# The first image's projection and convolution as a phase of their own in SBUF

## The chip, the cores and the metric

The kernel runs on one NeuronCore of one Trainium2 chip. The core has five engines that run side by side and wait for each other through semaphores: TensorE (PE), VectorE (DVE), ScalarE (ACT), GpSimd (POOL) and SyncE (SP), which here only issues DMAs. Each engine takes its own instructions strictly in the order in which the program gives them. The metric is device time in microseconds (us); the time before is the median of five runs.

## The reference

Two layers on an image batch x of 8 x 192 x 64 x 64 (float32). The second one is a window attention with an MLP and is not touched. The first, cut to what matters:

```
x = conv1x1(x, W_in)                          # 192 -> 384 channels
x = depthwise_conv3x3(x, W_dw) + b_dw         # each of the 384 channels by itself, 'SAME'
x_proxy = conv1x1(x, W_xd)                    # 384 -> 16
ws, Ls, Us, Ds = (conv1x1(x_proxy, w) for w in (W_w, W_l, W_u, W_d))
xs = concat of x, x transposed, and both flipped along W       # four directions
Gl, Gm, Gr = parts of ws, divided by the sum of their absolute values
out = gate_scan(xs, Ls, Gl, Gm, Gr, chunk=8)  # h = l*x + gl*h_up + gm*h + gr*h_dn, 8 steps
y = sum over directions of w_m * (out * Us + xs * Ds); layernorm; grn; conv1x1(y, W_out)
```

The change concerns the first two lines for image 0 alone.

## The kernel before, in words

All data are float32 and 128 partitions hold 128 channels: the 384 channels are three tiles, `ct` 0 to 2. An image is handled in three parts.

*front* (L526 to L641) makes the convolved image. It goes through the image in eight strips of eight rows (`s`). `read` (L530) loads two strips of x into `xt`. `project` (L541) multiplies by `w_in` on PE, ACT copies the result to `xin` (L561), and SP stores that to a zero-bordered copy of the image in DRAM, `pad` (L570). `convolve` (L575) loads `strip` tiles from `pad`, so that three image rows' worth of 32 channels lie on 96 partitions (L584), and PE multiplies them by the banded matrix `w_cv` (L596). ACT writes the outcome twice with the bias added: `st` (L610), in the order in which the forward scan takes its columns, and `sn` (L623), plain. SP stores them to two DRAM arrays, `xs` (L629) and `xsT` (L630). An image has 24 such blocks (3 tiles by 8 strips).

*scan* (L644 to L1041) takes one image in eight steps t. For each step `proxy` (L659) loads `x0` from `xs` (L662), multiplies by `w_xd` on PE (L669), copies (L679), sends the result to DRAM and back to spread it over the partitions (`flat` L684, `xe` L692), and copies it in the other order (`xo` L699). Then 12 tiles (four directions by three `ct`) are worked off by PE (gate products, L709), ACT (L766, L788, L810, L812), DVE (L742 at t = 0, later L758, L773, L775, L807, L825, L834, L842; outputs L868, L873) and POOL (L797, L814, L818, L829; sums L880, L882, L888, L890). Every step reads all of its image's `xs`; `xd` loads (L725) take columns of `xs` and `xsT`.

*windows* (L1563) is the second layer on the finished image.

The order is written out by a planner (`Plan`, L78 to L308). Each part declares its steps with an engine, a cost in ns, what it reads and writes, and a rank (a due time); `order` (L146) simulates the five engines 60 times with shifted ranks and keeps the shortest run; the instructions are then emitted in that order under a manual schedule (L1587 to L1592). The loop at L1577 gives the scan of image b, the windows of image b-1 and the front of image b+1 to the planner, so that they interleave; the front of image 0 has nothing beside it but the weights' preparation.

Before the planner's part stand the loads of weights (`load`, L332, on SP's and ACT's queues by turns), zeroed buffers (`blank`, L344, on DVE), the zero rows of `pad` (L398, SP) and the preparation of the weights (L403 to L476): `w_cv` (L408 to L410), `w_g2` by `w_m` (L419), `w_out` (L422 to L425), two bias rows (`bias_row`, L427, whose DMAs L431, L442 and L444 go by SP), `b_f1` and `w_f1` (L466 to L472), `rpb`. These lie outside of the manual schedule; there the framework's own scheduler orders them. L485 loads ACT's function table.

Of the kernel before, what the change touches and what calls it, by code (L numbers as in the profile page):

```python
# [23 lines left out]
F32 = mybir.dt.float32  # L24
U8 = mybir.dt.uint8
AF = mybir.ActivationFunctionType
ALU = mybir.AluOpType
AX = mybir.AxisListType
PSUM = bass.MemoryType.PSUM
DRAM = bass.MemoryType.DRAM  # L30

P = 128
B, DM, H, W = 8, 192, 64, 64
DIN, ND, NS = 384, 4, 16
CT = DIN // P
CH = 8
HEADS, HD, WS = 6, 32, 8
HALF = DM // 2
NG = H // WS
# [15 lines left out]
class Held:  # L55
# [5 lines left out]
        self.users, self.left, self.end, self.next, self.tile = [], 0, 0.0, None, None  # L61

    def make(self):
        pool, shape, dtype, name, tag, bufs = self.args
        self.tile = pool.tile(shape, dtype, name=name, tag=tag, bufs=bufs)

# [250 lines left out]
def tile_ss2d_then_window_attention(ctx: ExitStack, tc: tile.TileContext, a: dict, out: bass.AP):  # L317
# [6 lines left out]
    nc = tc.nc  # L324
    x = a["x"]
# [6 lines left out]
    def load(name, src=None, rows=None):  # L332

        nonlocal n_loads
        src = a[name] if src is None else src
        shape = list(src.shape)
        t = const.tile([rows or shape[0]] + shape[1:], F32, tag=name, name=name)
        if rows:
            nc.vector.memset(t[HALF:rows], 0.0)
        queues[n_loads % 2].dma_start(t[0 : shape[0]], src)  # L340
        n_loads += 1
        return t

    def blank(name, shape, value=None):  # L344
        t = const.tile(shape, F32, tag=name, name=name)
        if value is not None:
            nc.vector.memset(t, value)
        return t

    w_in = load("w_in")  # L350
    vecs = load("vecs")
    w_xd = load("w_xd")
    w_g1 = load("w_g1")
    w_g2 = load("w_g2")
# [12 lines left out]
    b_f1 = load("b_f1")  # L367
    w_f2 = load("w_f2")
    b_f2 = load("b_f2")
    b_dw, gamma, beta, ln_w, ln_b = (vecs[:, k, :] for k in range(5))  # L370
    n2_g, n2_b = (n2_gb[:, k, :] for k in range(2))

    ident = blank("ident", [P, P])
    make_identity(nc, ident)
    mean384 = blank("mean384", [P, RG], 1.0 / DIN)
    eps5 = blank("eps5", [P, 1], 1e-5)
    eps7 = blank("eps7", [P, 1], 1e-7)
    neg = blank("neg", [P, 1], NEG)
# [9 lines left out]
    xT = blank("xT", [P, 2, GT])  # L388
    sT, oT = (blank(n, [P, 2, GT], 0.0) for n in ("sT", "oT"))
    for t in (sT, oT):  # L390
        nc.vector.memset(t[HALF : HALF + 1, 1, :], 1.0)

    dram = ctx.enter_context(tc.tile_pool(name="dram", bufs=2, space=DRAM))

    pad = [dram.tile([DIN, H + 2, W + 2], F32, name=f"pad{k}", bufs=1) for k in range(2)]
    for k in range(2):
        for row in (0, H + 1):
            nc.sync.dma_start(  # L398
                pad[k][:, row, :].rearrange("(n p) w -> p n w", p=P), hid[0][0][:, 0 : CT * (W + 2)].rearrange("p (n w) -> p n w", n=CT)
            )  # L400


    with tc.tile_pool(name="prep", bufs=2) as prep, tc.tile_pool(name="prep_ps", bufs=2, space=PSUM) as prep_ps:  # L403

# [11 lines left out]
        for n, pair in enumerate(PAIRS):  # L416
            for k, (d, _) in enumerate(pair):
                w = w_g2[64 * k : 64 * k + 64, n * P : (n + 1) * P]
# [30 lines left out]
        for j in range(2):  # L449
            ps = prep_ps.tile([P, 512], F32, name="ps_pre")  # L450
            for ci in range(2):
                nc.tensor.matmul(
                    ps[0:HALF, 0:1],
                    lhsT=w_v[0:HALF, ci, j * HALF : (j + 1) * HALF],
                    rhs=n1_b[:, ci : ci + 1],
                    start=ci == 0,
                    stop=ci == 1,
# [5 lines left out]
        for m in range(NM):  # L463
            cols = slice(m * P, (m + 1) * P)
# [5 lines left out]
        for ci in range(2):  # L470
            w = w_f1[:, ci, :]
# [15 lines left out]
    plan = Plan()  # L487
# [1075 lines left out]
    def windows(b, z, made):  # L1563
        for g in range(NG):
            yield from window_row(b, g, z, *made[b])

    def written_down(b, lane, length, ahead, steps):

        plan.lane = lane
        k = 0  # L1570
        plan.rank = b - ahead
        for _ in steps:
            k += 1
            plan.rank = b + min(1.0, k / length) - ahead

    made, scans, sums = {}, {}, {}
    for b in range(-1, B + 1):  # L1577
        if 0 <= b < B:
            sums[b] = Held(dram, [P, CT, CH, 512], "z")
            written_down(b, 0, CH * 12 + 1, 0.4, scan(b, *scans[b], sums[b], made))  # L1580
        if 0 <= b - 1 < B:
            written_down(b, 1, NG * 25, 0.0, windows(b - 1, sums[b - 1], made))
        if b + 1 < B:
            scans[b + 1] = tuple(Held(dram, [P, CT, CH, 512], n, bufs=3) for n in ("xs", "xsT"))
            written_down(b, 2, CT * 12, 0.5, front(b + 1, *scans[b + 1]))

    kinds = mybir.EngineType  # L1587
    with tc.manual_schedule(engines={kinds.PE, kinds.Activation, kinds.DVE, kinds.Pool, kinds.SP}):
        for s in plan.order():
            for h in s.makes:  # L1590
                h.make()
            s.fn()  # L1592


def _laid_out(i):

    z = lambda *s: np.zeros(s, np.float32)
    f = lambda n: np.asarray(i[n])
    rows = lambda a, n: np.ascontiguousarray(a.reshape(-1, n, a.shape[-1]).transpose(1, 0, 2))
    cols = lambda a, n: np.ascontiguousarray(a.reshape(-1, n).T)  # L1600
    L0, L1 = "L0_conv_", "L1_conv_"

    w_xd = z(P, CT, RG)
    w_g1, w_g2 = z(P, ND * DIN), z(P, len(PAIRS) * P)
    w_xd[:, :, 0:NS] = rows(f(L0 + "W_xd").T, P)
    gates = f(L0 + "W_w").reshape(3, ND * DIN, NS)
    for r, w in enumerate([gates[0], gates[1], gates[2], f(L0 + "W_l")]):
        w_g1[RG * r : RG * r + NS] = w.T
    for n, pair in enumerate(PAIRS):
        for k, (d, ct) in enumerate(pair):  # L1610
            chs = slice(d * DIN + ct * P, d * DIN + (ct + 1) * P)
            for m, w in enumerate(("W_d", "W_u")):
                w_g2[64 * k + RG * m :][:NS, n * P : (n + 1) * P] = f(L0 + w)[chs].T


    qkv_w = f(L1 + "qkv_w").reshape(3, 3, 2, HD, DM).transpose(0, 2, 1, 3, 4)
    qkv_b = f(L1 + "qkv_b").reshape(3, 3, 2, HD).transpose(0, 2, 1, 3)
    proj = f(L1 + "proj_w").reshape(DM, 3, 2, HD).transpose(2, 1, 3, 0)

    at = np.stack(np.meshgrid(np.arange(WS), np.arange(WS), indexing="ij")).reshape(2, -1)  # L1620
    at = at.reshape(2, WS, WS).transpose(0, 2, 1).reshape(2, -1)
    rel = at[:, :, None] - at[:, None, :] + WS - 1
    rpb = f(L1 + "rpb_table")[rel[0] * (2 * WS - 1) + rel[1]]
    rpb = rpb.reshape(64, 64, 3, 2).transpose(3, 0, 2, 1).reshape(P, 3, 64)

    vec = [f(L0 + n) for n in ("b_dw", "grn_gamma", "grn_beta", "ln_w", "ln_b")]
    twice = lambda a: np.stack([a[0:P], np.concatenate([a[P:DM]] * 2)], 1)
    laid = {
        "x": f("x"),
        "w_in": twice(f(L0 + "W_in").T),  # L1630
        "w_dw": f(L0 + "W_dw").reshape(CT, 4, RG, 3, 3).transpose(3, 2, 0, 1, 4).reshape(3 * RG, CT * 12),
        "vecs": np.stack([cols(v, P) for v in vec], 1),
        "w_xd": w_xd,
        "w_g1": w_g1,
        "w_g2": w_g2,
        "w_m": f(L0 + "w_m"),
        "w_out": rows(f(L0 + "W_out").T, P),
        "w_qk": rows(qkv_w[:2].reshape(2 * DM, DM).T, HALF),
        "b_qk": qkv_b[:2].reshape(1, 2 * DM),
        "w_v": rows(qkv_w[2].reshape(DM, DM).T, HALF),  # L1640
        "b_v": cols(qkv_b[2].reshape(DM), HALF),
        "w_pr": rows(proj.reshape(DM, DM), HALF),
        "b_pr": f(L1 + "proj_b").reshape(1, DM),
        "n1_g": f(L1 + "norm1_g"),
        "n1_br": f(L1 + "norm1_b").reshape(1, DM),
        "n1_b": cols(f(L1 + "norm1_b"), HALF),
        "n2_gb": np.stack([twice(f(L1 + n)) for n in ("norm2_g", "norm2_b")], 1),
        "temp": f(L1 + "temperature").reshape(3, 2).T.reshape(HEADS),
        "rpb": rpb,
        "w_f1": twice(f(L1 + "fc1_w").T),  # L1650
        "b_f1": cols(f(L1 + "fc1_b"), P),
        "w_f2": rows(f(L1 + "fc2_w").T, P),
        "b_f2": twice(f(L1 + "fc2_b")),
    }
    return {k: np.ascontiguousarray(v) for k, v in laid.items()}
# [17 lines left out]
```

## Time and profile before

| what | value |
|---|---|
| median of 5 runs (lowest to highest) | 7635.64 us (7619.77 to 7638.28) |
| the profiled execution | 7638.28 us, span 7636.5 us |
| mean granted PE clock over the span | 0.862 |
| PE busy | 6713.8 us (88%) |
| DVE busy | 6283.7 us (82%) |
| POOL busy | 6212.1 us (81%) |
| ACT busy | 4887.9 us (64%) |

Times in a view of the trace count from the start of the span. A line of the timeline gives start, duration, engine, source line, operation, what is written and read, how often, and in brackets how long the engine had been idle and what ended that. "PEld" is PE loading weights and "SPq" SP issuing a DMA. A line of grouped instructions gives count, total and mean duration (ns), and then the idle time just before them with what ended most of it.

### The profile page before, as it was taken

The page shows a single profiled execution, that of the slowest core. Times are in us where ns is not written, and L with a number is a line of the kernel's source. Part 1 is how long each engine was busy: PE and PEld are TensorE (multiplying, and loading weights), DVE is VectorE, ACT ScalarE, POOL GpSimd, SP SyncE. Part 2 cuts the span into 40 slices and gives each one's busy share as a digit, 9 for nine tenths or more (in the row PEclk, how much of TensorE's full clock was granted, in tenths as well). Part 3 has the DMA queues.
Part 4 walks back from the last instruction along what each step waited for, and adds up shares of the span by engine and source line. Part 5 has one row for each costly group of instructions (what it writes and reads, how often), then busy time and mean ns, then how long its engine had stood idle before and what let it go on. Part 6 is the DMA issues. An engine that isn't in the chain of part 4 may idle for free.

```text
span 7636.5 us, 144071 instructions
## 1 busy us (share of the span) xinstructions
PE 6713.8 (88%) x51224; PEld 3465.8 (45%) x51224; DVE 6283.7 (82%) x15421; ACT 4887.9 (64%) x9657; POOL 6212.1 (81%) x6302
## 2 busy tenths in 40 slices
PE   6788888998998999899999899998888888888887
PEld 2333344444444444444444444444444444444554
DVE  1387889899899988899889979889899999999543
ACT  2355546776677666776677657767566656767665
POOL 0388989899899989888889979888889989899422
PEclk8788779988898889988899789988888788889998
DMA  7766545411552145411553135511211212111100
GB/s 189 186 174 164 137 117 139 122 50 58 147 146 74 47 117 134 126 48 51 139 151 86 43 89 148 134 48 50 61 49 43 58 52 59 45 49 48 30 22 14
DMA packets 1037924, 695.49 MB, mean 91 GB/s; under 512 B 704115, under 2 KB 860214, under 8 KB 1037206
## 3 DMA queue, kind: packets, MB, share of 16 engines
q1 hardware_dynamic: 1035830, 684.99, 33.8%
q8 instruction: 406, 6.65, 0.4%
q14 instruction: 312, 2.56, 0.1%
q10 hardware_dynamic: 1376, 1.30, 0.1%
HBM read 453.43 MB, written 232.67 MB: 90 GB/s over the span
## 4 chain that ended last, share of the span: by engine, by line
PE 22%; DVE 19%; POOL 14%; ACT 8%; issue 4%; DMA 1%; SPq 0%; POOLq 0%; ACTq 0%; DVEq 0%
PE g L709 7%; PE lp L1528 4%; POOL pw L829 2%; POOL ab L797 2%; POOL pw L814 2%; PE lp L1494 2%; POOL dx L882 2%; DVE rest L1281 2%; POOL pw L818 1%; DVE nb L807 1%; DVE nb L834 1%; PE lp L596 1%; PE lp L1137 1%; POOL y L890 1%; DVE dx L868 1%
## 5 line engine op out<-in xcount | busy, mean ns | idle before, releaser
L709 PE MATMUL g<-xo,w_g 32*128 32x512 f32 x3648 | 1232.0, 735 | 210.0 <-DVE dx L868 78.8
L709 PE MATMUL g<-xe,w_g 32*128 32x512 f32 x3648 | 1159.6, 749 | 170.2 <-DVE dx L868 46.1
L766 ACT ACTIVATE ab<-g 128x512 f32<-128x512 f32 x1344 | 781.2, 596 | 387.3 <-PE g L709 157.2
L797 POOL TENSOR_TENSOR ab<-ab 128x512 f32<-128x512 f32 x672 | 868.8, 1293 | 137.2 <-ACT ab L766 125.0
L829 POOL TENSOR_TENSOR pw<-pw,rr 128x512 f32<-128x512 f32 x672 | 867.0, 1290 | 132.9 <-ACT rr L812 107.5
L814 POOL TENSOR_TENSOR pw<-pw,pq 128x512 f32<-128x512 f32 x672 | 875.4, 1303 | 83.0 <-DVE pq L773 66.5
L818 POOL TENSOR_TENSOR pw<-pw,pq 128x512 f32<-128x512 f32 x672 | 874.0, 1301 | 14.6
L882 POOL TENSOR_TENSOR dx<-dx,hu 128x512 f32<-128x512 f32 x576 | 742.1, 1298 | 119.8 <-DVE hu L873 101.6
L810 ACT ACTIVATE rr<-nb,eps 128x512 f32<-128x512 f32 x672 | 460.6, 685 | 556.6 <-DVE nb L807 554.5
L596 PE MATMUL lp<-strip,w_cv 128*32 128x256 f32 x9216 | 669.7, 432 | 114.0 <-DMA strip<-pad 103.6
L709 PEld LDWEIGHTS g<-xo,w_g 32*128 32x128 f32 x3648 | 417.8, 208 | 759.9 <-DVE dx L868 184.8
L709 PEld LDWEIGHTS g<-xe,w_g 32*128 32x128 f32 x3648 | 407.1, 212 | 651.9 <-DVE dx L868 136.0
L1528 PE MATMUL lp<-hd,w_f 128*64 128x256 f32 (+1 forms) x2304 | 578.9, 488 | 45.6 <-ACT hd L1514 15.3
L890 POOL TENSOR_TENSOR y<-y,dx 128x512 f32<-128x512 f32 x384 | 598.6, 1565 | 2.1
L825 DVE SCALAR_TENSOR_TENSOR nb<-nb,rr 128x512 f32<-128x512 f32 x672 | 466.3, 694 | 124.0 <-ACT rr L812 121.8
L834 DVE SCALAR_TENSOR_TENSOR nb<-nb,pw 128x512 f32<-128x512 f32 x672 | 466.0, 694 | 120.9 <-POOL pw L829 118.8
L880 POOL TENSOR_TENSOR y<-hu,dx 128x512 f32<-128x512 f32 x192 | 249.6, 1305 | 379.2 <-DMA xsT<-sn 278.3
L807 DVE TENSOR_TENSOR nb<-nb,ab 128x512 f32<-128x512 f32 x672 | 466.6, 694 | 107.9 <-POOL ab L797 100.4
L596 PEld LDWEIGHTS lp<-strip,w_cv 128*32 128x32 f32 x9216 | 299.0, 121 | 503.2 <-issue 262.1
L873 DVE TENSOR_TENSOR hu<-g,hid 128x512 f32<-128x512 f32 x768 | 521.0, 684 | 5.6 <-PE g L709 4.3
L788 ACT ACTIVATE nb<-nb 128x512 f32<-128x512 f32 x672 | 399.2, 594 | 160.5 <-DVE pq L773 87.1
L709 PE MATMUL nb<-xe,w_g 32*128 32x512 f32 x672 | 477.7, 797 | 19.7 <-DVE hid L842 19.3
(205 smaller groups left out, 16688.0 us busy)
## 6 DMA issues: line engine op xcount, KB each, us to landing
strip<-pad SPq DMA_DIRECT2D x1152, 132.0 KB
xd<-xsT SPq DMA_DIRECT2D x384, 256.0 KB
pad<-xin SPq DMA_DIRECT2D x192, 264.0 KB
xsT<-sn SPq DMA_DIRECT2D x192, 256.0 KB
xs<-st SPq DMA_DIRECT2D x192, 256.0 KB
xd<-xs SPq DMA_DIRECT2D x192, 256.0 KB
x<-xs SPq DMA_DIRECT2D x64, 768.0 KB
z<-y SPq DMA_DIRECT2D x64, 768.0 KB
```

The source lines that it names most:

```text
L596: nc.tensor.matmul(pc()[q * RG : (q + 1) * RG, k * 256 : (k + 1) * 256].rearrange("p (h w) -> p h w", h=4), lhsT=w_cv[:, ct, q, dx, :], rh ...
L709: nc.tensor.matmul(dst, lhsT=w[rows, col : col + P], rhs=xp[rows, :], start=True, stop=True)
L766: lambda r=r: nc.scalar.activation(ab()[:, r, :], g[r](), AF.Abs),
L797: plan("POOL", gp(512), lambda: nc.gpsimd.tensor_add(ab()[:, 0, :], ab()[:, 0, :], ab()[:, 1, :]), w=[ab])
L807: plan("DVE", vec(512), lambda: nc.vector.tensor_add(nb(), nb(), ab()[:, 0, :]), r=[ab], w=[nb])
L814: plan("POOL", gp(512), lambda: nc.gpsimd.tensor_add(one(), one(), pq()[:, 0, :]), r=[(pq, 0)], w=[pw])
L818: lambda: nc.gpsimd.tensor_add(one(), one(), pq()[:, 1, :]),
L829: plan("POOL", gp(512), lambda: nc.gpsimd.tensor_mul(one(), one(), rr()), r=[rr], w=[pw])
L834: lambda: nc.vector.scalar_tensor_tensor(nb(), nb(), 2.0, one(), ALU.subtract, ALU.mult),
L882: plan("POOL", gp(512), lambda: nc.gpsimd.tensor_add(dx(), dx(), hu()), r=[hu], w=[dx])
L890: nc.gpsimd.tensor_add(y, y, dx().rearrange("p (c i) -> p i c", c=CH))
L1528: nc.tensor.matmul(dst[:, at : at + rhs.shape[-1]], lhsT=lhsT, rhs=rhs, **flags)
```

## The change

Image 0 leaves the planner. Its front is written out by hand as a phase that runs before everything else but the loads:

- All of image 0's x is loaded into two tiles, `xa` (channels 0 to 127) and `xb` (the other 64, in two halves of the partitions), in four units of 16 rows, on SP (`xa`) and ACT (`xb`); all weight loads but `w_in`, `w_dv` (the nine taps as a scalar per channel, a new input) and `vecs` come after these.
- `projected` does the product with `w_in` for 16 rows and copies them into `full[ct]`, an image of 66 x 66 with zero borders, in SBUF.
- `convolved` does a block of 16 rows on DVE: one tensor_scalar with the bias, eight multiply-adds onto `acc`.
- `convolved_by_products` does it on PE: nine products with a diagonal matrix `dg` for each half of the block, summed in PSUM, then ACT adds the bias.
- `stored` copies a block into `sn` and `st` on ACT and stores them; blocks are twice as high as before, so a store carries 512 KB and not 256.
- Of 12 blocks, nine go to DVE (ct 0, ct 1, and the first of ct 2), three to PE (the rest of ct 2).

The zeroing of buffers moves from DVE to POOL. The manual schedule now covers the whole program, the weights' preparation too, which keeps its place in the text and so follows the phase on each engine. The planner starts with scan 0 and has seven fronts.

```diff
-            nc.vector.memset(t[HALF:rows], 0.0)
+            nc.gpsimd.memset(t[HALF:rows], 0.0)
...
-    def blank(name, shape, value=None):
+    def blank(name, shape, value=None, engine=nc.gpsimd):
...
-            nc.vector.memset(t, value)
+            engine.memset(t, value)
...
+    ctx.enter_context(tc.manual_schedule(engines={kinds.PE, kinds.Activation, kinds.DVE, kinds.Pool, kinds.SP}))
...
+    ident = blank("ident", [P, P])
+    make_identity(nc, ident)
+
     w_in = load("w_in")
-    vecs = load("vecs")
+    w_dv = load("w_dv")
+    xa = epool.tile([P, H, W], F32, name="xa")
+    xb = epool.tile([P, NG // 2, 8, W], F32, name="xb")
+    for u in range(NG // 2):
+        nc.sync.dma_start(xa[:, 16 * u : 16 * u + 16, :], x[0, 0:P, 16 * u : 16 * u + 16, :])
+        for k in range(2):
+            row = 16 * u + 8 * k
+            nc.scalar.dma_start(xb[64 * k : 64 * k + 64, u], x[0, P:DM, row : row + 8, :])
+        if u == 0:
+            vecs = load("vecs")
+    full = [epool.tile([P, H + 2, W + 2], F32, name=f"full{ct}") for ct in range(CT)]
+    for t in full:
+        nc.vector.memset(t[:, 0 : H + 2 : H + 1, :], 0.0)
+        nc.vector.memset(t[:, :, 0 : W + 2 : W + 1], 0.0)
...
+    with early, tc.tile_pool(name="early_ps", bufs=2, space=PSUM) as early_ps:
...
+        def projected(ct, u):
+            cols = slice(ct * P, (ct + 1) * P)
+            pin = early_ps.tile([P, 16, W], F32, name="pin")
+            outs = [pin[:, 8 * k : 8 * k + 8, :] for k in range(2)]
+            for k in range(2):
+                row = 16 * u + 8 * k
+                nc.tensor.matmul(outs[k], lhsT=w_in[:, 0, cols], rhs=xa[:, row : row + 8, :], start=True, stop=False)
+            for k in range(2):
+                half = slice(64 * k, 64 * k + 64)
+                nc.tensor.matmul(outs[k], lhsT=w_in[half, 1, cols], rhs=xb[half, u], start=False, stop=True)
+            nc.scalar.copy(full[ct][:, 16 * u + 1 : 16 * u + 17, 1 : W + 1], pin)
+
+        def stored(ct, u, acc):
+            cols = slice(128 * u, 128 * u + 128)
+            xs, xsT = scans[0]
+            st, sn = (epool.tile([P, CH, 2, 64], F32, name=n, bufs=3) for n in ("st", "sn"))
+            nc.scalar.copy(sn.rearrange("p t k w -> p k t w"), acc.rearrange("p (k t) w -> p k t w", k=2))
+            nc.sync.dma_start(xsT()[:, ct, :, cols], sn.rearrange("p t k w -> p t (k w)"))
+            for k in range(2):
+                rows = acc[:, 8 * k : 8 * k + 8, :]
+                nc.scalar.copy(
+                    st[:, :, k, :].rearrange("p t (r c) -> p r c t", c=CH), rows.rearrange("p r (c t) -> p r c t", t=CH)
+                )
+            nc.sync.dma_start(xs()[:, ct, :, cols], st.rearrange("p t k w -> p t (k w)"))
+
+        def near(ct, u, dy, dx):
+            return full[ct][:, 16 * u + dy : 16 * u + dy + 16, dx : dx + W]
+
+        def convolved(ct, u):
+            acc = epool.tile([P, 16, W], F32, name="acc", bufs=3)
+            for n, tap in enumerate(taps):
+                w = w_dv[:, ct, n : n + 1]
+                if n == 0:
+                    nc.vector.tensor_scalar(acc, near(ct, u, *tap), w, b_dw[:, ct : ct + 1], ALU.mult, ALU.add)
+                else:
+                    nc.vector.scalar_tensor_tensor(acc, near(ct, u, *tap), w, acc, ALU.mult, ALU.add)
+            stored(ct, u, acc)
+
+        def convolved_by_products(ct, u):
+            acc = epool.tile([P, 16, W], F32, name="acc", bufs=3)
+            for k in range(2):
+                pc = early_ps.tile([P, CH, W], F32, name="pc")
+                for n, (dy, dx) in enumerate(taps):
+                    row = 16 * u + 8 * k + dy
+                    nc.tensor.matmul(
+                        pc, lhsT=dg[:, n, :], rhs=full[ct][:, row : row + 8, dx : dx + W], start=n == 0, stop=n == 8
+                    )
+                nc.scalar.activation(acc[:, 8 * k : 8 * k + 8, :], pc, AF.Identity, bias=b_dw[:, ct : ct + 1])
+            stored(ct, u, acc)
+
+        for n in range(9):
+            nc.scalar.activation(dg[:, n, :], ident, AF.Copy, scale=w_dv[:, CT - 1, n : n + 1])
+        units = [(ct, u) for ct in range(CT) for u in range(NG // 2)]
+        by_vector = [(ct, u) for ct, u in units if ct < CT - 1 or u == 0]
+        by_tensor = [c for c in units if c not in by_vector]
+        done = 0
+        for ct, u in units:
+            projected(ct, u)
+            while done < len(by_vector) and by_vector[done] < (ct, u):
+                convolved(*by_vector[done])
+                done += 1
+            while by_tensor and by_tensor[0] < (ct, u):
+                convolved_by_products(*by_tensor.pop(0))
+        for c in by_tensor:
+            convolved_by_products(*c)
...
+    plan("SP", (0.0, 0.0), lambda: None, w=scans[0])
...
-            written_down(b, 2, CT * 12, 0.5, front(b + 1, *scans[b + 1]))
+            if b >= 0:
+                written_down(b, 2, CT * 12, 0.5, front(b + 1, *scans[b + 1]))
```

More of the change, by code (lines that the diff above doesn't have):

```diff
@@ L63, in make @@
     def make(self):
+        if self.tile is not None:
+            return
         pool, shape, dtype, name, tag, bufs = self.args
@@ L342, in load @@
         return t
-    def blank(name, shape, value=None):
+    def blank(name, shape, value=None, engine=nc.gpsimd):
         t = const.tile(shape, F32, tag=name, name=name)
         if value is not None:
-            nc.vector.memset(t, value)
+            engine.memset(t, value)
         return t
-    w_in = load("w_in")
-    vecs = load("vecs")
+    kinds = mybir.EngineType
+    ctx.enter_context(tc.manual_schedule(engines={kinds.PE, kinds.Activation, kinds.DVE, kinds.Pool, kinds.SP}))
+    dram = ctx.enter_context(tc.tile_pool(name="dram", bufs=2, space=DRAM))
+    scans = {b: tuple(Held(dram, [P, CT, CH, 512], n, bufs=3) for n in ("xs", "xsT")) for b in range(B)}
+    early = ExitStack()
+    epool = early.enter_context(tc.tile_pool(name="early", bufs=1))
+    ident = blank("ident", [P, P])
+    make_identity(nc, ident)
+    w_in = load("w_in")
+    w_dv = load("w_dv")
[12 more added lines that the diff above has]
+        nc.vector.memset(t[:, :, 0 : W + 2 : W + 1], 0.0)
+    b_dw = vecs[:, 0, :]
     w_xd = load("w_xd")
@@ L369, in tile_ss2d_then_window_attention @@
     b_f2 = load("b_f2")
-    b_dw, gamma, beta, ln_w, ln_b = (vecs[:, k, :] for k in range(5))
+    gamma, beta, ln_w, ln_b = (vecs[:, k, :] for k in range(1, 5))
     n2_g, n2_b = (n2_gb[:, k, :] for k in range(2))
-    ident = blank("ident", [P, P])
-    make_identity(nc, ident)
     mean384 = blank("mean384", [P, RG], 1.0 / DIN)
@@ L390, in tile_ss2d_then_window_attention @@
     for t in (sT, oT):
-        nc.vector.memset(t[HALF : HALF + 1, 1, :], 1.0)
-    dram = ctx.enter_context(tc.tile_pool(name="dram", bufs=2, space=DRAM))
+        nc.gpsimd.memset(t[HALF : HALF + 1, 1, :], 1.0)
     pad = [dram.tile([DIN, H + 2, W + 2], F32, name=f"pad{k}", bufs=1) for k in range(2)]
@@ L400, in tile_ss2d_then_window_attention @@
             )
+    for h in scans[0]:
+        h.make()
+    with early, tc.tile_pool(name="early_ps", bufs=2, space=PSUM) as early_ps:
+        taps = [(dy, dx) for dy in range(3) for dx in range(3)]
+        dg = epool.tile([P, 9, P], F32, name="dg")
+        def projected(ct, u):
[58 more added lines that the diff above has]
+            convolved_by_products(*c)
+        assert done == len(by_vector)
@@ L1574, in written_down @@
             plan.rank = b + min(1.0, k / length) - ahead
-    made, scans, sums = {}, {}, {}
+    made, sums = {}, {}
+    plan("SP", (0.0, 0.0), lambda: None, w=scans[0])
     for b in range(-1, B + 1):
@@ L1583, in tile_ss2d_then_window_attention @@
         if b + 1 < B:
-            scans[b + 1] = tuple(Held(dram, [P, CT, CH, 512], n, bufs=3) for n in ("xs", "xsT"))
-            written_down(b, 2, CT * 12, 0.5, front(b + 1, *scans[b + 1]))
[L1587 to L1592, printed above, removed]
+            if b >= 0:
+                written_down(b, 2, CT * 12, 0.5, front(b + 1, *scans[b + 1]))
+    for s in plan.order():
+        for h in s.makes:
+            h.make()
+        s.fn()
 def _laid_out(i):
@@ L1630, in _laid_out @@
         "w_in": twice(f(L0 + "W_in").T),
+        "w_dv": rows(f(L0 + "W_dw").reshape(DIN, 9), P),
         "w_dw": f(L0 + "W_dw").reshape(CT, 4, RG, 3, 3).transpose(3, 2, 0, 1, 4).reshape(3 * RG, CT * 12),
```

## The prediction

> **What bounds the kernel now.** I read the page's forty slices first, then busy time by stretch around the start, then the waits of the first 400 us, then the timeline there.
>
> ```profile
> DVE  1387889899899988899889979889899999999543
> POOL 0388989899899989888889979888889989899422
> ```
>
> One slice is 191 us. VectorE and GpSimd are near nine tenths from the third slice on and almost idle in the first and half of the second: a start stage that only PE, ACT and the DMAs work in.
>
> ```profile
> 27.15:248.07 220.92, 141.06 (x1284) 64.09 (x1280) 3.71 (x17) 54.56 (x74) 0.00 (x0) 0.80 0.77 195
> 248.07:275.88 27.81, 18.74 (x141) 7.96 (x144) 0.00 (x0) 5.98 (x10) 0.00 (x0) 0.69 0.61 165
> 275.88:960.00 684.12, 583.58 (x3998) 245.55 (x3995) 530.88 (x837) 360.31 (x615) 583.33 (x461) 0.78 0.61 161
> ```
>
> Busy us of PE, PE loads, DVE, ACT, POOL, then clock, DMA share, GB/s. In the first stretch (image 0's front) DVE works 3.7 of 221 us, while the DMA engines are 0.77 busy with the trip through the padded copy in DRAM. Only after 275.88 do the scan's engines fill up.
>
> ```profile
> POOL y L880 <- DMA xsT<-sn: 278.3, 1, 278.3
> DVE hid L742 <- PE g L709: 250.4, 4, 241.3
> ```
>
> Both scan engines sit through one wait of 240 to 280 us. It is exposed from end to end.
>
> ```profile
> 244.53 0.37 SPq L629 DMA_DIRECT2D xs<-st  x1
> 248.07 0.60 SPq L662 DMA_DIRECT2D x<-xs  x1
> ...
> 260.01 0.64 SPq L684 DMA_DIRECT2D flat<-xq  x1
> ...
> 263.19 0.57 SPq L692 DMA_DIRECT2D xe<-flat  x1
> ...
> 275.88 0.69 DVE L742 TENSOR_TENSOR hid<-g,x 128x512 f32<-128x512 f32 x1 [241.35 <-PE g L709]
> ```
>
> The last store of image 0, the first load of the scan 3.5 us later, then 27.8 us of proxy chain to the first scan product. That chain and all behind it stay. So the change is worth the move of one event, the issue of the scan's first x0 load, at **248.07 us** now.
>
> **Rows that price the new phase.** VectorE:
>
> ```profile
> 1013.58 0.70 DVE L834 SCALAR_TENSOR_TENSOR nb<-nb,pw 128x512 f32<-128x512 f32 x1 [2.45 <-POOL pw L829]
> 1014.31 0.69 DVE L842 TENSOR_TENSOR hid<-lx,nb 128x512 f32<-128x512 f32 x1
> 1014.92 0.68 DVE L868 TENSOR_TENSOR dx<-g,xd 128x512 f32<-128x512 f32 x1
> 1015.52 0.68 DVE L873 TENSOR_TENSOR hu<-g,hid 128x512 f32<-128x512 f32 x1
> ```
>
> Independent 512-wide operations start 0.60 us apart; L842 needs L834's result and starts 0.73 after it. Another 512 elements cost 0.53 us (L926, 1536 wide, takes 1.751 against 0.694: 1.057 for 1024). A tap is 1024 wide and adds onto the tap before it: 0.73 + 0.53 = 1.26 us. Bounds: 1.13 as if independent; 1.31 with an allowance of 0.05 for the scalar read per partition, which no row isolates.
>
> The Trainium skill, "VectorE: DVE Perf Modes", section Terms, has the pipe emptied after every operation before the next may issue. The row contradicts it for independent operations, 0.60 apart at 0.68 long. By the rule a tap would take its whole 1.22 us, or 0.04 us less than I take; over 72 taps 3 us less.
>
> The first tap has one tensor source. L472 halves its rate per element (768 in 0.60, 192 in 0.30): 1024 in 0.73, taken 0.75.
>
> ```profile
> 40.88 0.50 PEld L550 LDWEIGHTS lp<-xt,w_in 128*128 128x128 f32 x2 [0.81 <-issue]
> 41.90 0.34 PEld L550 LDWEIGHTS lp<-xt,w_in 128*128 128x128 f32 x1 [0.52 <-issue]
> ...
> 238.78 0.30 PEld L550 LDWEIGHTS lp<-xt,w_in 128*128 128x128 f32 x2 [0.41 <-ACT sn L623]
> 239.32 0.19 PEld L550 LDWEIGHTS lp<-xt,w_in 128*128 128x128 f32 x1 [0.24 <-issue]
> ```
>
> A 128x512 product is two passes. Loads of one kind come 0.85 us apart after idle time and 0.43 in busy stretches, so a product takes 1.71 (slow) to 0.86 us (fast).
>
> ```profile
> L610 ACT ACTIVATE st<-lp,vecs 128x512 f32<-128x512 f32 x192 | 223.0, 1162 | 72.3 <-PE lp L596 64.6 <-issue 4.7 <-ACT xin L561 1.8
> L699 ACT COPY xo<-xe 128x512 f32<-128x512 f32 x64 | 70.1, 1096 | 28.6 <-PE g L709 18.3 <-DMA xe<-flat 10.0
> ```
>
> The turned copy, 512 wide, costs ACT 1.1 us from PSUM or SBUF. A plain 1024-wide copy: 1.05 (L561's 0.59 plus 512 more at the 0.45 that L931's 1536 wide, 1.487 us, implies).
>
> **Removed.** Image 0's 24 blocks of front, with their strip, pad and store DMAs: all the time from 27.15 to 248.07.
>
> **Added, in order.**
> *Loads.* Before, of 20 loads each waited for the eighth before it (w_v at 4.19 although SP was free, temp at 10.7 for w_out), the last on ACT near 11.9. Now there are 33, ACT issues 18 of them ahead of its first activation, and the last of these waits for the 24th to land, 5.7 MB. The first 12 us moved 218 GB/s, single 3 us stretches up to 401: 26 or 14 us; with tails 15 to 30, I take 24. Then a table load 1.3 (L485), nine 128-wide diagonals 2.3 (L679, 0.27 busy), one copy 1.0: VectorE's first tap at 28.7.
> *VectorE.* Eight blocks of ct 0 and 1 and one of ct 2: a block is 8 x 1.26 + 0.75 = 10.8; nine, 97.5 (88 to 102). End at 126.2.
> *Does it stall between blocks?* ACT's order is copy(u+1), then the three store copies of block u, which wait for block u's last tap. Block u+1's taps 7 to 9 need copy(u+2), queued behind them: 1.05 + 2.2 + 1.05 = 4.3 us. Its first six taps need no new row and last 7 us, so with waits by rows this is covered. SP shows such precision on DRAM: xd<-xs was issued at 239.44, ahead of stores to other channels of xs.
> *TensorE's quarter does not run beside VectorE.* Its units are the last three. Copy(2,1) stands behind the stores of block (1,3), so products begin at 126.2 - 10.8 + 4.3 = 119.7: 54 x 0.86 = 46.4, 1.7 for two at the slow rate, 3.0 for the last projection. End 170.8 (all slow: 46 more). ACT 3.9 and an issue 0.4: last store at 175.1.
> *The preparation is now behind it.* Before, it hid under the front (DVE 17 to 35 us, in the scheduler's own order). Now each engine takes it after the phase, and SP must issue the two bias rows before any x0 load; behind those rows sit x0, front 1's xt, every DMA. w_dw issue to use 5.2 (16.98 to 22.14), then on DVE w_cv 1.35, twelve L419 3.4, L422 to L425 1.7, add 0.5, store issue 0.6, the second row's load 3, its adds 0.7, store issue 0.5: 17.4 (5 if all but the tail overlaps, 22 at most). x0 load issued at **192.5**; sum of the bounds 160 to 225.
> *Moved at no cost.* DVE's memsets (14 us before 17.2) go to GpSimd, which has 278 us of nothing to do; if they were late they would hold SP's pad zeroing, some microseconds. 12.6 MB of stores over 140 us are 90 GB/s, half of what the front drew.
> *What is late next.* Front 1 began 36.5 us ahead of x0 (xt at 211.57) and now cannot; its last store is at 899.96 and scan 1's x0 load at 955.10, so 55 us cover it. Beyond that each us would cost one.
>
> Sum: 248.1 - 192.5 = 55.6 us. The profiled execution took 7638.28 (span 7636.5), giving 7582.7; the runs' median is 2.6 lower, so **7580**, with 7547 to 7612 as this case's own range.
>
> **Rivals.**
> *Waits by whole tile.* Then every block waits out the 4.3 us plus hops: 8 x 4.5 = 36 us back, **7616**. For it: ACT's queue order. Against: the SP row above.
> *The phase is shorter.* Loads at the 401 GB/s rate, taps at 1.13, preparation overlapped: x0 load near 160, **7548**. For it: DVE alone in SBUF. Against: the chained adds.
> *Slower: the new order of the other seven images.* The planner searches 60 orders of all steps; without front 0 the search runs a different course. From 1000 to 6400 us PE, DVE and POOL are 0.88 to 0.90 busy, the remainder is order (L825 alone waits 122 us for ACT). If the found order idles 1.6 points more over 5400 us, 86 us are lost: **7666**. It decides from 10 us an image on (56 + 15 over seven). For it: nothing holds the order still. Against: same steps, costs and choice of the best of 60, so it may as well gain; no row shows the scatter.
> *It is hidden anyway*: front 1 becomes the wait and eats the gain, about **7635**; against, the 55 us margin.
>
> **Numbers.** Forecast 0.60, shorter phase 0.13, whole-tile waits 0.12, slower order 0.10, hidden 0.05. This kernel's measurements tell 0.2% apart, 7620 to 7651. X. The range reaches from 7530 (below the short phase, with a lucky order) to 7640; it leaves out the slower order and little below.
>
> **What would show it.** Right: x0 load near 192; tap starts 1.26 apart without a gap at tap 7; DVE idle some 50 us between its last tap and the preparation, PE filling it; POOL's first wait near 225; stretches from 1000 us on as busy as now. Wrong: gaps of 4 us in every block; w_dw loaded early; PE's quarter at 1.7 us a product; an x0 load moved as said with a span that did not follow, which would be the order.

## The result, and the profile after

| | before | changed |
|---|---|---|
| median, us | 7633.43 (45 runs) | 7627.9 (25 runs) |
| ratio, 95% interval | | 0.9996 (0.9989 to 1.0002) |
| span of the profiled execution, us | 7636.5 | 7631.5 |
| issue of the first x0 load, us | 248.07 | 199.20 |

No difference that can be measured, where 7580 was forecast. Yet the event on which the forecast was built, the issue of the first x0 load, did move. Forty slices of the changed kernel, the two scan engines:

```profile
DVE  5677788998899988988888888889899989889643
POOL 0688888998899988988888888989899989899422
```

VectorE works in the first slice now, and GpSimd's third digit and those after it are on the whole no fuller than before. Stretches of the changed kernel (columns as before): loads, VectorE's blocks, TensorE's tail, preparation, proxy chain, scan.

```profile
0.00:26.00 26.00, 7.55 (x17) 2.51 (x17) 0.98 (x7) 5.02 (x12) 14.78 (x37) 0.82 0.92 280
26.00:128.20 102.20, 51.71 (x84) 17.15 (x85) 99.04 (x81) 31.15 (x34) 0.00 (x0) 0.66 0.32 86
128.20:180.20 52.00, 46.62 (x114) 19.75 (x112) 0.00 (x0) 18.58 (x21) 0.00 (x0) 0.97 0.29 81
180.20:199.20 19.00, 10.31 (x35) 8.01 (x36) 9.93 (x30) 0.00 (x0) 0.00 (x0) 0.50 0.15 44
199.20:222.26 23.06, 14.27 (x92) 5.66 (x93) 0.00 (x0) 4.51 (x8) 0.00 (x0) 0.66 0.53 158
222.26:960.00 737.74, 610.80 (x4143) 251.40 (x4140) 567.71 (x896) 382.39 (x649) 627.21 (x496) 0.79 0.58 156
```

VectorE is 99 of 102 us busy, then idle for 52 while PE finishes. The timeline of the joints:

```profile
25.93 0.82 DVE L468 TENSOR_SCALAR acc<-full,w_dv,vecs 128x1024 f32<-128x1024 f32 x1 [23.79 <-DMA w_f<-in_w_f_dram]
26.78 10.60 DVE L470 SCALAR_TENSOR_TENSOR acc<-full,w_dv,acc 128x1024 f32<-128x1024 f32 x8
37.30 0.81 DVE L468 TENSOR_SCALAR acc<-full,w_dv,vecs 128x1024 f32<-128x1024 f32 x1
...
141.77 31.17 PE L480 MATMUL pc<-full,dg 128*128 128x512 f32 x72
...
180.23 0.19 DVE L508 TENSOR_TENSOR id<-ident 96x32 f32<-96x32 f32 x1 [52.13 <-DMA xs<-st]
...
199.20 0.59 SPq L762 DMA_DIRECT2D x<-xs  x1
...
222.26 0.69 DVE L842 TENSOR_TENSOR hid<-g,x 128x512 f32<-128x512 f32 x1 [23.09 <-PE g L809]
```

Blocks follow each other every 11.4 us (25.93 to 37.30) without a hole at tap 7, and the scan's first product starts at 222.26, 53.6 us ahead of the kernel before (275.88). So 49 to 54 us were gained by 222 us and 5 were left at the end of the span: **some 44 us went missing in a part of the program whose steps are the same.** The issue of x0 loads shows where the lead goes. First image 4's, then image 5's and image 7's, in the kernel before:

```profile
3550.62 0.62 SPq L662 DMA_DIRECT2D x<-xs  x1
...
4387.05 0.62 SPq L662 DMA_DIRECT2D x<-xs  x1
...
6146.41 0.56 SPq L662 DMA_DIRECT2D x<-xs  x1
```

and in the changed one:

```profile
3465.67 0.56 SPq L762 DMA_DIRECT2D x<-xs  x1
...
4378.16 0.55 SPq L762 DMA_DIRECT2D x<-xs  x1
...
6131.37 0.56 SPq L762 DMA_DIRECT2D x<-xs  x1
```

At image 4 the scans are 85 us ahead, at image 5 only 9. The scans' lead says little alone, because the windows run between them; here is the last output store of image 2's windows for the first 128 channels, before and changed:

```profile
3933.68 0.36 SPq L1554 DMA_DIRECT2D out_dram<-ot  x1
```

```profile
4040.64 0.34 SPq L1654 DMA_DIRECT2D out_dram<-ot  x1
```

107 us later: at this point the changed kernel is ahead with the scans and behind with the windows, so neither event alone says how far the whole has come.

The planner computes a length for the order that it finds (no time of the chip): 7453 us before, of which 7165 lie behind the x0 load, and 7177 changed, of which 7173 do. By its own account the new order is 8 us longer behind that load; on the chip the same stretch is 7631.5 - 199.2 = 7432 against 7636.5 - 248.1 = 7388, 44 us longer.

### The profile page after: what moved, and what is told of

The parts are those of the page before. It is cut to its first block, busy times and chain, and to the rows that moved or that the text cites. A ratio compares the mean times of both kernels' runs of the same rounds, so it can differ in the third digit from the quotient of the medians.

```text
span 7631.5 us, 141764 instructions
## 1 busy us (share of the span) xinstructions
PE 6711.8 (88%) x50180; PEld 3455.8 (45%) x50180; DVE 6361.9 (83%) x15477; ACT 4892.0 (64%) x9649; POOL 6222.3 (82%) x6333
## 5 line engine op out<-in xcount | busy, mean ns | idle before, releaser
L809 PE MATMUL g<-xo,w_g 32*128 32x512 f32 x3648 | 1195.2, 730 | 189.9 <-DVE dx L968 90.9
L1628 PE MATMUL lp<-hd,w_f 128*64 128x256 f32 (+1 forms) x2304 | 598.1, 498 | 57.7 <-ACT hd L1614 15.0
L696 PE MATMUL lp<-strip,w_cv 128*32 128x256 f32 x8064 | 563.6, 418 | 23.7 <-DMA strip<-pad 18.9
L809 PE MATMUL nb<-xo,w_g 32*128 32x512 f32 x672 | 466.6, 780 | 15.7 <-DVE hid L942 15.7
```

Of the source, the lines that this page charges most:

```text
L696: nc.tensor.matmul(pc()[q * RG : (q + 1) * RG, k * 256 : (k + 1) * 256].rearrange("p (h w) -> p h w", h=4), lhsT=w_cv[:, ct, q, dx, :], rh ...
L809: nc.tensor.matmul(dst, lhsT=w[rows, col : col + P], rhs=xp[rows, :], start=True, stop=True)
L1628: nc.tensor.matmul(dst[:, at : at + rhs.shape[-1]], lhsT=lhsT, rhs=rhs, **flags)
```

## The experiments

Medians of different experiments are not set against each other, because the kernel before, timed beside each of them, had medians from 7633 to 7639 itself; the ratios are, each taken against the kernel before as timed beside it.

Two theories. **A**: the phase gives its 49 us, and the order that the planner found for the remaining work loses them. **B**: something in the rest (an engine's load, DMA traffic, front 1's later start) takes up any gain at the start.

**e1, the new phase with the old order.** The planner is given all eight fronts, as before; front 0's steps are left out when the order is written out. The order of all other steps is then that of the kernel before, step for step.

```diff
-    plan("SP", (0.0, 0.0), lambda: None, w=scans[0])
+    skipped = set()
...
-            if b >= 0:
-                written_down(b, 2, CT * 12, 0.5, front(b + 1, *scans[b + 1]))
+            known = len(plan.steps)
+            written_down(b, 2, CT * 12, 0.5, front(b + 1, *scans[b + 1]))
+            if b < 0:
+                skipped.update(plan.steps[known:])
...
+        if s in skipped:
+            continue
```

> The new phase, but everything behind it in the order of the kernel before: the planner is given front 0 too and its steps are left out when the instructions are written. Theory A (the phase gives its 49 us and the newly found order of the other work loses 45 of them): the first x0 load stays near 199 us, the rest takes what it took before (7636.5 - 248 = 7388), together near 7587, a ratio of 0.993 to 0.995. Theory B (something in the rest, an engine's load, DMA traffic or front 1's later start, takes up any gain at the start): 7625 to 7635, ratio 0.999 to 1.000.

Measured: 7591.19, ratio **0.9936** (0.9922 to 0.9950). Its x0 loads of images 0, 4 and 7:

```profile
207.77 0.60 SPq L762 DMA_DIRECT2D x<-xs  x1
...
3503.67 0.62 SPq L762 DMA_DIRECT2D x<-xs  x1
...
6093.26 0.57 SPq L762 DMA_DIRECT2D x<-xs  x1
```

The lead over the kernel before is 40, 47 and 53 us: it stays. (The first one is 9 us later than in the changed kernel because the old order puts more of front 1 ahead of it: besides the four loads of x that both orders issue first, two stores to `pad` and six loads of `strip`.) The same store of image 2's windows is 40 us ahead too, at 3893.41. Theory B falls.

**e2, the old front with the new order.** The kernel before, with front 0 planned by itself and emitted first, and the rest planned as in the changed kernel.

```diff
+    written_down(-1, 2, CT * 12, 0.5, front(0, *scans[0]))
+    emit()
+    plan = Plan()
...
+    plan("SP", (0.0, 0.0), lambda: None, w=scans[0])
...
+            if b >= 0:
+                written_down(b, 2, CT * 12, 0.5, front(b + 1, *scans[b + 1]))
```

> The opposite swap: front 0 as before, planned by itself, then the rest in the order that the changed kernel found. Theory A: x0 load at 240 to 250, then the 7432 us that the changed kernel takes from there: 7672 to 7682, ratio 1.005 to 1.007. Theory B: 7630 to 7640, ratio 1.000.

Measured: 7677.41, ratio **1.0047** (1.0034 to 1.0060), x0 load at 250. The order by itself costs 36 us. Both swaps came out as A has them.

**e3 and e4, neighbouring orders.** The changed kernel with two other tries of its own search.

```diff
-            if best is None or self.length < best[0]:
+            if n == 42:
```

(59 in e4.)

> The changed kernel with the order of the search's 43rd try, whose planned length is 3 us above the best (7180 against 7177). Theory A: the time from the x0 load to the end differs from that of the best order by tens of us, so 7590 to 7670, with no telling which way. Theory B: within 5 us of the changed kernel, 7623 to 7633.

> The changed kernel with the order of the 60th try, planned 10 us longer than the best (7187). Theory A: 7590 to 7680, not in step with the planned lengths. Theory B: 7628 to 7643, the changed kernel plus at most the planned 10 us.

Measured: 7640.35, ratio 0.9997 (0.9985 to 1.0009), and 7641.74, 0.9998 (0.9988 to 1.0008): the same as the changed kernel's 0.9996 within the intervals. Two tries of one search may well resemble each other, so they do not tell whether the loss is that of this search or of any search; "tens of us" was too much for such neighbours.

**e5 to e8, other searches.** One constant of the planner is changed by a trifle, `SLACK` 40 to 41 ns or `HOP` 35 to 36, which sends the search another way and alters no step of the program: in the kernel before (e5, e6) and in the changed one (e7, e8). Theories L and S are those of the first expectation below.

> The kernel before with one constant of the planner's search changed (SLACK 41 ns for 40): no step, cost or tile differs, only the order found, whose planned length is 7484 us against 7453. Theory L (the outcome of the search is a draw that scatters by tens of us, and the order of the kernel before is a good one): 7650 to 7690, ratio 1.002 to 1.007. Theory S (taking front 0 out of the plan leads the search to worse orders for a reason, and with front 0 in it any search does as well as the kernel before): 7628 to 7648, ratio 0.999 to 1.001.

> The kernel before with HOP 36 ns for 35, planned length 7508 us against 7453. Theory L: 7660 to 7710, ratio 1.003 to 1.010. Theory S: 7628 to 7648.

> The changed kernel with SLACK 41, planned 7180 us against 7177 for the changed kernel. Theory L: another draw of the same lottery, 7590 to 7670. Theory S: 7620 to 7645.

> The changed kernel with HOP 36, planned 7184 us. Theory L: 7590 to 7680, and over e7 and e8 the changed kernels lie below e5 and e6 by about 50 us, the gain of the phase when draws of like quality are compared. Theory S: 7620 to 7645, no lower than e5 and e6 by more than 15 us.

| search | front 0 in the plan | changed kernel |
|---|---|---|
| as given | 7636.11, 1 | 7627.9, 0.9996 (0.9989 to 1.0002) |
| SLACK 41 | 7656.44, 1.0027 (1.0015 to 1.0040) | 7633.44, 0.9994 (0.9983 to 1.0005) |
| HOP 36 | 7716.96, 1.0099 (1.0082 to 1.0116) | 7626.63, 0.9989 (0.9978 to 0.9999) |

One nanosecond in a constant makes the kernel before 20 and 81 us slower: its order was the best of the three drawn. All five orders of the changed kernel lie between 0.9989 and 0.9998. By the ratios of the table the changed kernel is 3, 25 and 84 us the faster, 37 in the mean, near the phase's 49, but three draws that scatter by 80 us don't fix that mean. Theory S falls with e5 and e6, which it had at 7628 to 7648, and with e7 and e8, which it had no more than 15 us below them. Theory L took the order before for a good one and had e7 and e8 about 50 us below e5 and e6; they are 57 below in the mean of the medians. That the changed kernel's times lie so close together, S had and L had not. The planner's own lengths, in the expectations above, go along with this: 31 and 55 us longer than the order before for e5 and e6, and within 10 us of each other for all five orders of the changed kernel.

**e9 and e10, a shorter phase.** The weights' preparation is emitted behind the first two projections instead of behind the phase, and TensorE's blocks are started in VectorE's third block, half a block at a time; e9 has the old order (as e1), e10 the changed kernel's own.

```diff
+        projected(0, 0)
+        projected(0, 1)
...
+        halves = [(2, u, k) for u in (1, 2, 3) for k in range(2)]
+        more = {0: [(2, 0), (2, 1)], 1: [(2, 2), (2, 3)]}
+        for i, c in enumerate(by_vector):
+            taken(*c)
+            if i:
+                stored(*by_vector[i - 1], acc_of.pop(by_vector[i - 1]))
+            if 2 <= i + 2 < 8:
+                projected(*by_vector[i + 2])
+            for m in more.get(i, ()):
+                projected(*m)
+            if going:
+                half_out(*going)
+                going = None
+            if i >= 2 and halves:
+                h = halves.pop(0)
+                going = (*h, half(*h))
```

> e1 (the order of the kernel before) with a shorter phase: the weights' preparation ahead of the blocks instead of behind them, and TensorE's three blocks started in VectorE's third block, half a block at a time, instead of last. VectorE's first tap near 36 us, its last near 138, x0 load near 145 instead of 208. If a gain at the start passes to the end when the order is held: 145 + 7371 (e1's time from there) = 7516, up to 7533 with the 7388 of the kernel before; ratio 0.984 to 0.987. If front 1, which now starts 50 us later against the scan than in the kernel before, becomes the wait, or the rest takes up an earlier start: 7560 to 7591, ratio 0.990 to 0.994.

> The same shorter phase with the changed kernel's own order. If its order costs a fixed 45 us or so, whatever the start: 145 - 199 = 54 us below the changed kernel, 7570 to 7580, ratio 0.991 to 0.993. If this order makes the rest wait for something that the phase does not move (DMA, front 1), then 7600 to 7630.

Measured: e9 **7546.15, ratio 0.9882** (0.9867 to 0.9897), the fastest of all; e10 7593.13, 0.9938 (0.9925 to 0.9950). Neither reached its number, because the x0 load did not come as early as I said. VectorE and the x0 load in e9:

```profile
30.36 1.35 DVE L525 TENSOR_TENSOR w_cv<-id,w_dw 96x1152 f32<-96x1152 f32 x1 [27.97 <-DMA w_dw<-in_w_dw_dram]
...
45.85 0.16 DVE L584 TENSOR_TENSOR b_f<-b_f,ps_pre 128x6 f32<-128x6 f32 x1 [5.44 <-PE ps_pre L581]
...
47.65 0.81 DVE L495 TENSOR_SCALAR acc<-full,w_dv,vecs 128x1024 f32<-128x1024 f32 x1
...
167.98 0.60 SPq L799 DMA_DIRECT2D x<-xs  x1
```

The preparation waited for `w_dw` until 30.36 and then for PE, so the first tap came at 47.65 and not at 36. That is 12 of the 23 us by which e9's x0 load missed 145; the other 11 are the steps of front 1 that the old order puts ahead of it, as in e1 (in e10 it came at 157). The x0 load moved from 207.8 to 168.0, 40 us, and the time by 0.0054 of the kernel before, 41 us; in e10 it moved from 199 to 157, 42 us, and the time by 0.0058, 44 us. With the order held, what the start gains arrives at the end, within the 10 us or so that these runs leave open, with either order. Front 1 did not become the wait.

The two differ in the order alone, so they price it a third time: 0.9938 against 0.9882, 43 us. Their mean granted TensorE clock is the same, 0.863 over the runs of each, so the clock does not account for it.

## Why the prediction was wrong

*What bounds the start, and what the phase costs:* right. The x0 load was put at 192.5 and came at 199.20, a little luckily, as an early first tap made up for part of what came late behind it. Term by term: first tap 28.7, came at 25.93 (26 us of loads at 280 GB/s, not 218); nine blocks 97.5, took 102.2, because a tap starts 1.315 us after the one before it ((37.30 - 26.78) / 8), at the bound of 1.31 that allows for the per-partition scalar and not at 1.26 (that the scalar is the reason, no run isolates); TensorE's end 170.8, came at 172.9, 36 products in 31.17 us being 0.87 each; preparation from the last store's issue to the x0 load 17.4 (its terms add up to 16.95), took 22.6. The chain that was priced, up to the second row's store, took 16.1; then came front 1's four loads, 2.4, and a wait of SP for VectorE's last step of the preparation, which the sum did not have:

```profile
SPq L762 <- DVE rpb L576: 3.9, 1, 3.9
```

No stall at tap 7, so *waits by whole tile* fell.

*Moved at no cost:* right. GpSimd's zeroing was done by 15.6 us, and front 1's later start cost nothing that can be measured (e1, e9).

*The step that failed* is the one in "The sum": 248.1 - 192.5 = 55.6 us taken off the whole time, with all work behind the x0 load taken to last as long as before ("That chain and all behind it stay"). It lasts 44 us longer, and the sign that the prediction named for this, an x0 load moved as said with a span that did not follow, is what came. The rival that I had for this, **the new order of the other seven images**, is what happened: I gave it 0.10 and priced it at 86 us, and the swaps price it at 36 (e2), 43 (e10 against e9) and 46 (the changed kernel against e1, 0.0060 of 7634). The argument against it, that steps, costs and choice are the same and it may as well gain, treated the order before as a middling draw. e5 and e6 show it to be the best of three, so a new search had more to lose than to gain. The page showed no scatter of orders, as the prediction says; the range should then have been set by that unknown and not by the phase's bounds.

*Still open.* Whether leaving front 0 out of the plan makes the search's orders worse as such was not settled: it would take many draws of both. The few draws do not speak for it. From the x0 load to the end of the span the profiled executions took 7388, 7395 and 7477 us with front 0 in the plan (the kernel before, e5, e6) and 7432, 7437 and 7431 without it (changed, e7, e8), so these lie between the others. Open too is why the chip falls further behind the plan in one order than in the other (by 260 us over the changed kernel's rest, 223 over the old one's, the planned x0 and end against those of the trace); no single wait accounts for it. The busy times of e1 and then of the changed kernel, from 3200 to 5200 us, show where the scans lose their lead:

```profile
3200.00:4200.00 1000.00, 918.33 (x6990) 472.33 (x6986) 895.60 (x2102) 687.36 (x1366) 887.20 (x892) 0.88 0.34 92
4200.00:5200.00 1000.00, 894.88 (x7065) 460.42 (x7066) 884.27 (x2176) 676.37 (x1326) 884.02 (x881) 0.88 0.33 91
```

```profile
3200.00:4200.00 1000.00, 911.40 (x7050) 471.37 (x7043) 870.98 (x2174) 684.16 (x1355) 865.00 (x878) 0.89 0.34 91
4200.00:5200.00 1000.00, 912.76 (x7197) 482.73 (x7194) 877.92 (x2154) 684.59 (x1363) 865.82 (x883) 0.88 0.34 92
```

GpSimd is busy 40 us less in the changed kernel (887.20 + 884.02 against 865.00 + 865.82) and VectorE 31 less; PE and the DMAs do as much as in e1. In this stretch the scans' lead over the kernel before shrinks from 85 us to 9. But the windows catch up in it: their last store for the first 128 channels of image 3, before and changed, comes 52 us early, after 107 us late for image 2:

```profile
4956.18 0.34 SPq L1554 DMA_DIRECT2D out_dram<-ot  x1
```

```profile
4904.47 0.36 SPq L1654 DMA_DIRECT2D out_dram<-ot  x1
```

So scan work was in part exchanged for window work here, and where the 44 us are lost is not shown.

## What to carry to other kernels

Where a search writes the order of the instructions, any edit to what it is given is also a new draw of the order: here a nanosecond in a constant moved the time by 20 and 81 us, where the edit by itself was worth 49 (e1). Measure an edit with the order held still, and then draw several orders; the order at hand may be a lucky one, as here, and a new one then gives back some of it. A stage at the start that nothing covers is worth what it lasts, but only in that comparison.

## What the runs showed of the hardware that was not expected

A 1024-wide multiply-add on VectorE with a scalar read per partition, each on the result of the one before, started every 1.315 us, 0.05 above what the 512-wide rows gave. Each lasted 1.285 us, so it began after the one before had ended, where independent 512-wide operations overlap (0.60 apart at 0.68 long). The memsets that went from VectorE to GpSimd took no longer there (128x1056: 1.90 us for two against 1.88). And the 24 one-column products of the preparation took PE 6.27 us at a granted clock of 0.50 (the stretch 180.20 to 199.20), where the kernel before had done them in 3.80, at 0.99 over these us.
